# Row sums of attention weights: eight of sixteen key tiles summed on VectorE before TensorE

## The chip, the cores and the metric

One core of a Trainium2 chip runs the whole kernel. The metric is device time in microseconds (us), the median of three runs; lower is better. The engines named here are TensorE (PE; its weight loads are shown apart as PEld), VectorE (DVE), ScalarE (ACT), GpSimd (POOL), and SyncE (SP), whose queue issues all the kernel's DMAs.

## The reference

Eight entries (b), each of 2048 nodes with 256 features, go through two graph attention layers, each followed by a residual addition and a layer norm. In layer 0 there are 8 heads of 32 features:

```
e    = leaky_relu(e_src[i] + e_dst[j], 0.2) + softplus(beta) * log(adj + 1e-6)
attn = softmax over j of e, where adj[i, j] > 0
h    = attn @ x_proj                     (per head)
x    = layernorm(x + h @ W_out.T)
```

Layer 1 is dot-product attention on the result:

```
e = leaky_relu((x W1) (x W2).T, 0.2), masked by adj
x = layernorm(x + relu(softmax(e) @ (x W3)))
```

All data is float32. The softmax of layer 0 needs two things for each query i and head: the sum over all keys j of weight times value, and the sum over all keys of the weights alone, by which the first is divided.

## The kernel before

**Layer 0** (class `Gat`). Keys j are tiled by 128, so there are 16 key tiles (`jt`). Heads are taken in pairs (`hp`), so an entry has 4 passes of 16 key tiles, 64 units of work. In one unit (`step`) the mask-and-prior tile `mt` (128 keys by 2048 queries) is loaded; for each of the two heads VectorE makes a tile `s` = max(c, r) * mt, 128 x 2048, in one instruction (line 286); TensorE then multiplies `s` twice (line 294). With the values `v` as weights it adds to `val`, with the key's factor `e`, spread over 32 columns, it adds to `den`, the row sums. Each product is 128 x 32 by 128 x 512[...]; a unit has 8 for `val` and 8 for `den`. A float32 product appears as two instructions in the profile. `val` and `den` lie in PSUM over the whole pass. After the last key tile `finish` copies them out on ScalarE (lines 308 and 310), sends the row sums through DRAM to invert them (`rc`, `rec_d`) and to spread them (`rb`), and multiplies `ht` by them on VectorE (line 323), once for two passes.

**Buffers.** `s` has 4 tiles, that is two units; `mt` has 2, `c` has 3. The tag `d` has 2 tiles, which in the loop only `rb` uses (the adjacency tiles use it in entry 0).

**Layer 1** (class `Dot`). Queries are tiled by 128, so an entry has 16 dot steps. A step transposes the softmax tile `p` (line 404, copied by ScalarE to `pts`, line 406), makes the scores `e` of the next step (line 385), which ScalarE passes through Prelu into `p` (line 387), VectorE masks and reduces (line 390) and ScalarE exponentiates (line 391), and accumulates `acc` (line 420). Then `rec`, `z` and the layer norm follow. Every fourth step also makes the queries `h1` (`h1p`, line 374). The PSUM tiles of `e`, `pt` and the others are 3 in all; `acc` has one.

**The order.** The main loop runs layer 1 of one entry beside layer 0 of the next, and the order of TensorE is the order of the code. Units are put between the pieces of other work: 4 in `output` (layer 0's last product and its layer norm, by query tile), 8 in `turn` (transposes and `h3`), 4 in dot step 0 and then 4, 4, 3, 4, 4, 3, ... in dot steps 1 to 13:

```
dot.step(lambda k: layer_0((2, 1, 1)[k]))
for i in range(NT - 3):
    dot.step(lambda k: layer_0((0, 2 - (i % 3 == 2), 2)[k]))
```

Here k = 0 stands at the start of the step, 1 after the scores and 2 after `acc`. Dot steps 14 and 15 run at the start of the next round, with `project` of the following entry. So pass 0 of an entry lies in `output`, `turn` and dot step 0, and passes 1 to 3 in dot steps 1 to 13. Entry 0 has no layer 1 beside it; entry 7's layer 1 ends the program alone. The order on the other engines and on SP's queue is fixed when the program is built, by the tile framework's scheduler[...].

Of the kernel before, what the change touches and what calls it, by code (L numbers as in the profile page):

```python
# [9 lines left out]
F32 = mybir.dt.float32  # L10
BF16 = mybir.dt.bfloat16
I32 = mybir.dt.int32
AF = mybir.ActivationFunctionType
ALU = mybir.AluOpType
# [4 lines left out]
P = 128  # L19
# [8 lines left out]
def kernel(  # L28
# [26 lines left out]
    nc = tc.nc  # L55
    B, N, D = x.shape
    H, _, DH = w_proj.shape
    NT = N // P
    KC = D // P
    BK = 512  # L60
    NB = N // BK
    HALF = N // 2
    HP = 2
    NP = H // HP
    IG = BK // P

    const = ctx.enter_context(tc.tile_pool(name="const", bufs=1))
    dram = ctx.enter_context(tc.tile_pool(name="dram", bufs=1, space=DRAM))
# [7 lines left out]
    def mm_tile(name):  # L76
        return ps.tile([P, BK], F32, tag="mm", name=name)

    def wide_tile(name, tag, bufs, dtype=F32):
        return wide.tile([P, N], dtype, tag=tag, name=name, bufs=bufs)  # L80
# [7 lines left out]
    make_identity(nc, ident)  # L88
    eps_prior = const.tile([P, 1], F32)
    nc.vector.memset(eps_prior, PRIOR_EPS)  # L90
    eps_ln = const.tile([P, 1], F32)
    nc.vector.memset(eps_ln, LN_EPS)

# [61 lines left out]
    def make_mt(jt):  # L155

        a = wide.tile([P, NT, P], I32, tag="d", name="adj_t", bufs=2)
        nc.sync.dma_start(a, adj[:, ts(jt, P)].rearrange("(t p) j -> p t j", p=P))
        m = wide.tile([P, NT, P], F32, tag="p", name="m", bufs=2)
        nc.vector.tensor_scalar(m, a, 0.0, None, ALU.max)  # L160
        nc.scalar.activation(m, m, AF.Ln, bias=eps_prior)
        nc.scalar.activation(m, m, AF.Exp, scale=beta_c)
        nc.vector.scalar_tensor_tensor(m, a, 0.0, m, ALU.is_gt, ALU.mult)
        mt = wide_tile("mt", "mt", 2)
        for g in range(NB):
            t = mm_tile("mtp")
            for k in range(IG):
                nc.tensor.transpose(t[:, ts(k, P)], m[:, g * IG + k, :], ident)
            nc.scalar.copy(mt[:, ts(g, BK)], t)
        nc.sync.dma_start(mt_d[ts(jt, P), :], mt)  # L170
        return mt

    def load_mt(jt):
        mt = wide_tile("mt", "mt", 2)
        nc.sync.dma_start(mt, mt_d[ts(jt, P), :])
        return mt
# [25 lines left out]
    class Gat:  # L202
# [8 lines left out]
        def project(self):  # L211
# [8 lines left out]
            def turn(g):  # L220
                xr = chunk.tile([P, IG, D], F32, tag="xr", name="xr", bufs=1)
                nc.sync.dma_start(xr, xb[:, ts(g, IG), :])
                xt = chunk.tile([P, KC, BK], F32, tag="ht", name="xt", bufs=3)
                for kc in range(KC):
                    t = mm_tile("tr")
                    for k in range(IG):
                        nc.tensor.transpose(t[:, ts(k, P)], xr[:, k, ts(kc, P)], ident)  # L227
                    nc.scalar.copy(xt[:, kc, :], t)
                xts.append(xt)

            turn(0)
            for g in range(NB):
                if g + 1 < NB:
                    turn(g + 1)
                for k in range(IG):
                    it = g * IG + k
# [33 lines left out]
        def step(self, count=1):  # L270

            for _ in range(count):
                hp, jt = next(self.units)
                if jt == 0:
                    self.cs = [self.query_rows(hp * HP + a) for a in range(HP)]
                    self.val = pacc.tile([P, HALF], F32, tag="val", name="val")
                    self.den = pacc.tile([P, HALF], F32, tag="den", name="den")
                first = self.b == 0 and hp == 0
                while first and len(self.mts) < min(jt + 2, NT):
                    self.mts.append(make_mt(len(self.mts)))  # L280
                mt = self.mts[jt] if first else load_mt(jt)
                s = []
                for a in range(HP):
                    h = hp * HP + a
                    sa = wide_tile("s", "s", 4)
                    nc.vector.scalar_tensor_tensor(sa, self.cs[a], self.r[:, jt, h:h + 1], mt, ALU.max, ALU.mult)  # L286
                    s.append(sa)
                for dst in (self.val, self.den):
                    for c in range(HALF // BK):
                        for q in range(4):  # L290
                            h = hp * HP + q % 2
                            w = (self.v[:, jt, ts(h, DH)] if dst is self.val
                                 else self.e[:, jt, h:h + 1].to_broadcast([P, DH]))
                            nc.tensor.matmul(dst[ts(q, DH), ts(c, BK)], w,  # L294
                                             s[q % 2][:, ds(q // 2 * HALF + c * BK, BK)],
                                             start=(jt == 0), stop=(jt == NT - 1))
                if jt == NT - 1:
                    self.finish(hp)

        def finish(self, hp):  # L300


            b, lo = self.b, hp % 2 * HP * DH
            if lo == 0:
                self.hts.append(whole.tile([P, N], F32, name=f"ht{hp // 2}"))
            ht = self.hts[-1]
            for s in range(2):
                nc.scalar.copy(ht[lo:lo + HP * DH, ts(s, HALF)], self.val[ts(s, HP * DH), :])  # L308
            dn = chunk.tile([P, HALF], F32, tag="xr", name="dn", bufs=1)
            nc.scalar.copy(dn, self.den)  # L310
            rc = small.tile([P, HALF // DH], F32, name="rc", bufs=1)
            for q in range(4):
                nc.sync.dma_start(rc[ts(q, DH), :], dn[q * DH:q * DH + 1, :])
            nc.vector.reciprocal(rc, rc)
            nc.sync.dma_start(rec_d[b, hp].rearrange("q (p c) -> (q p) c", c=HALF // DH), rc)
            if lo == 0:
                return
            rb = wide_tile("rb", "d", 2)
            for a in range(2 * HP):
                src = rec_d[b, hp - 1 + a // HP, a % HP::HP, :]  # L320
                nc.sync.dma_start(rb[ts(a, DH), :].rearrange("p (s i) -> p s i", s=2),
                                  bass.AP(tensor=src.tensor, offset=src.offset, ap=[[0, DH]] + list(src.ap)))
            nc.vector.tensor_mul(ht, ht, rb)
# [176 lines left out]
```

## Time and profile before

| | |
|---|---|
| median of 3 runs | 4947.42 us (4947.27 to 4948.94) |
| profiled execution, its own time | 4950.43 us |
| its span, first to last instruction | 4948.7 us |
| mean granted TensorE clock | 0.965 |
| PE busy | 4550.1 us, 92% |
| DVE busy | 3042.8 us, 61% |
| ACT busy | 1671.8 us, 34% |
| DMA | 166 GB/s mean, 47.6% of 16 engines' span |

A line of the costliest groups gives source line, engine, operation, the tile written and those read, their shapes and the number of instructions; then busy time, the mean of one in ns, and the idle time of the engine just before them with what ended most of it. A line of a timeline gives the start, the length in us, then engine, line, operation and number of instructions merged, and in brackets the idle time before it and what ended it. Matmuls are pipelined, so that one's length overlaps the next's start; their pace is read from start to start.

### The profile page before, as it was taken

Reading aid. Unit: us, or ns where it says so; the run is one execution under the profiler, and the core shown is the slowest. Engines: PE = TensorE matmul, PEld = TensorE weight load, DVE = VectorE, ACT = ScalarE, POOL = GpSimd, SP = SyncE. Lnnn points to the kernel's source line nnn. Section 1 sums busy time; section 2 is a strip of 40 time slices with the busy share of each in tenths; the row PEclk is TensorE's granted clock in tenths of the full one; section 3 lists DMA queues with packets and bytes.
Section 4 is the critical chain, followed back from the end, with each engine's and each line's share of the span. In section 5 each row is a group of like instructions: output and inputs, shape, how many; then the busy total and the mean of one; then the engine's idle time right before and its main releaser. Section 6 shows DMA issues by size and latency. Waiting matters only on the chain. (4 is left out here: it accounts for less than half of the span.)

```text
span 4948.7 us, 64738 instructions
## 1 busy us (share of the span) xinstructions
PE 4550.1 (92%) x27164; PEld 2315.8 (47%) x27164; DVE 3042.8 (61%) x2316; ACT 1671.8 (34%) x3683; POOL 3.6 (0%) x14
## 2 busy tenths in 40 slices
PE   6777899988999799997999889998899979999899
PEld 3211444453544444544444444445444444444566
DVE  5888666647666376664676556664666637666222
ACT  5300333333333333334333333333333333333454
POOL 0000000000000000000000000000000000000000
PEclk8899899999999899998999999999999989999999
DMA  7787445435454455444554445443545435444111
GB/s 217 253 307 258 168 169 177 174 103 200 168 179 169 135 177 179 173 161 142 175 179 167 141 159 178 169 171 119 183 171 181 172 130 184 168 174 164 53 50 43
DMA packets 249013, 821.08 MB, mean 166 GB/s; under 512 B 33424, under 2 KB 150416, under 8 KB 172944
## 3 DMA queue, kind: packets, MB, share of 16 engines
q1 hardware_dynamic: 248720, 816.93, 47.6%
q8 instruction: 213, 3.49, 0.3%
q14 instruction: 80, 0.66, 0.0%
HBM read 756.55 MB, written 59.77 MB: 165 GB/s over the span
## 5 line engine op out<-in xcount | busy, mean ns | idle before, releaser
L286 DVE SCALAR_TENSOR_TENSOR s<-c,r,mt 128x2048 f32<-128x2048 f32 x1024 | 2349.5, 2345 | 447.7 <-PE den L294 348.4
L294 PE MATMUL val<-s,v 128*32 128x512 f32 x8192 | 1085.6, 614 | 163.3 <-DVE s L286 155.1
L294 PE MATMUL den<-s,e 128*32 128x512 f32 x8192 | 1047.2, 599 | 8.6 <-ACT dn L310 8.6
L420 PE MATMUL acc<-h,pts 128*128 128x256 f32 x4096 | 948.6, 380 | 2.3 <-ACT pts L406 2.3
L385 PE MATMUL e<-x1t,h 128*128 128x512 f32 x2048 | 904.3, 595 | 0.0
L420 PEld LDWEIGHTS acc<-h,pts 128*128 128x128 f32 x4096 | 749.2, 190 | 89.2 <-ACT pts L406 4.2
L294 PEld LDWEIGHTS val<-s,v 128*32 128x32 f32 x8192 | 245.4, 111 | 800.7 <-issue 525.2
L390 DVE CUSTOM_DVE_ANT_0 p<-p,pen 128x2048 f32<-128x2048 f32 x128 | 293.4, 2292 | 501.2 <-ACT p L387 501.2
L406 ACT COPY pts<-pt 128x512 f32<-128x512 f32 x512 | 298.2, 584 | 878.9 <-PE pt L404 878.2
L385 PEld LDWEIGHTS e<-x1t,h 128*128 128x128 f32 x2048 | 380.2, 191 | 449.6 <-issue 422.5
L294 PEld LDWEIGHTS den<-s,e 128*32 128x32 f32 x8192 | 286.7, 112 | 639.3 <-issue 621.2
L387 ACT ACTIVATE p<-e 128x512 f32<-128x512 f32 x512 | 305.4, 596 | 539.5 <-PE e L385 539.5
L428 DVE TENSOR_TENSOR z<-z,x1r 128x256 f32<-128x256 f32 x128 | 54.5, 426 | 482.3 <-ACT z L427 482.3
L404 PEld LDWEIGHTS pt<-ident,p 128*128 128x128 f32 x2048 | 239.6, 141 | 211.5 <-issue 176.7
L391 ACT ACTIVATE p<-p,neg 128x2048 f32<-128x2048 f32 x128 | 256.8, 2006 | 234.5 <-DVE neg L390 234.3
L404 PE MATMUL pt<-ident,p 128*128 128x128 f32 x2048 | 317.5, 278 | 5.2 <-ACT p L391 5.2
L355 PE MATMUL h3p<-w3s,x1t 128*128 128x256 f32 x512 | 147.1, 411 | 41.3 <-ACT x1t L351 41.3
L427 ACT ACTIVATE z<-acc,rec 128x256 f32<-128x256 f32 x128 | 60.6, 473 | 354.7 <-PE acc L420 354.7
L192 ACT ACTIVATE f<-mv,eps_ln 128x1 f32<-128x1 f32 x256 | 74.3, 290 | 309.8 <-DVE mv L190 309.2
L308 ACT COPY ht<-val 64x1024 f32<-64x1024 f32 x64 | 64.2, 1003 | 305.4 <-PE val L294 305.0
L357 ACT COPY h<-h3p 128x256 f32<-128x256 f32 x128 | 47.5, 371 | 318.4 <-PE h3p L355 287.4
L227 PE MATMUL tr<-ident,xr 128*128 128x128 f32 x256 | 47.6, 348 | 105.2 <-DMA xr<-in_x_dram 104.6
(76 smaller groups left out, 2027.0 us busy)
## 6 DMA issues: line engine op xcount, KB each, us to landing
mt<-mt_d SPq DMA_DIRECT2D x496, 1024.0 KB, 4.8
c<-c_d SPq DMA_DIRECT2D x64, 1024.0 KB, 6.2
pen<-pen_d SPq DMA_DIRECT2D x128, 512.0 KB, 3.4
xr<-in_x_dram SPq DMA_DIRECT2D x32, 512.0 KB, 3.9
adj_t<-in_adj_dram SPq DMA_DIRECT2D x16, 1024.0 KB, 7.1
h<-in_x_dram SPq DMA_DIRECT2D x32, 512.0 KB, 4.6
mt_d<-mt SPq DMA_DIRECT2D x16, 1024.0 KB, 5.4
adj_r<-in_adj_dram SPq DMA_DIRECT2D x16, 1024.0 KB, 8.3
```

The lines of the kernel that those rows point to most:

```text
L192: nc.scalar.activation(f[:, 0:1], mv[:, 1:2], AF.Ln, bias=eps_ln)
L286: nc.vector.scalar_tensor_tensor(sa, self.cs[a], self.r[:, jt, h:h + 1], mt, ALU.max, ALU.mult)
L294: nc.tensor.matmul(dst[ts(q, DH), ts(c, BK)], w, s[q % 2][:, ds(q // 2 * HALF + c * BK, BK)], start=(jt == 0), stop=(jt == NT - 1))
L308: nc.scalar.copy(ht[lo:lo + HP * DH, ts(s, HALF)], self.val[ts(s, HP * DH), :])
L355: nc.tensor.matmul(t[:, 0:D], x1t[:, kc, ts(it, P)], w3s[:, kc, :], start=(kc == 0), stop=(kc == KC - 1))
L385: nc.tensor.matmul(t, self.h1[:, kc, ts(it % IG, P)], self.x1t[:, kc, ts(c, BK)], start=(kc == 0), stop=(kc == KC - 1))
L387: nc.scalar.activation(p[:, ts(c, BK)], t, AF.Prelu, alpha=ALPHA)
L390: nc.vector.tensor_tensor_reduce(p, p, pen, -1.0, FMAX, ALU.add, ALU.min, neg)
L391: nc.scalar.activation(p, p, AF.Exp, bias=neg, scale=-1.0, accum_out=den)
L404: nc.tensor.transpose(t[:, ts(k, P)], p[:, ts(g * IG + k, P)], ident)
L406: nc.scalar.copy(pt, t)
L420: nc.tensor.matmul(acc, now[:, ts(k, P)], self.h3[:, j, :], start=(j == 0), stop=(j == NT - 1))
```

## The change

In entries 1 to 7 the row sums of key tiles 2 to 9 of every pass are no longer formed by TensorE tile by tile. For tile 2, ScalarE writes `s` times the key's factor `e` into a tile `d` for each head; for tiles 3 to 9, VectorE adds `s` times `e` to it, in place. At key tile 11, after that tile's own products, one row-sum product with a weight tile of ones takes the two sums into `den`. Tiles 0, 1 and 10 to 15 keep their row-sum product, and entry 0 keeps all. The two sum tiles come from the tag `d`, which `rb` uses too.

```diff
+    SUMMED = range(2, 10)
...
+    ones = const.tile([P, DH], F32)
+    nc.vector.memset(ones, 1.0)
...
-                for dst in (self.val, self.den):
-                    for c in range(HALF // BK):
-                        for q in range(4):
-                            h = hp * HP + q % 2
-                            w = (self.v[:, jt, ts(h, DH)] if dst is self.val
-                                 else self.e[:, jt, h:h + 1].to_broadcast([P, DH]))
-                            nc.tensor.matmul(dst[ts(q, DH), ts(c, BK)], w,
-                                             s[q % 2][:, ds(q // 2 * HALF + c * BK, BK)],
-                                             start=(jt == 0), stop=(jt == NT - 1))
+                v, e = self.v, self.e
+                heads = [hp * HP + a for a in range(HP)]
+                self.products(self.val, jt, [v[:, jt, ts(h, DH)] for h in heads], s)
+                if self.b > 0 and jt in SUMMED:
+                    if jt == SUMMED[0]:
+                        self.sums = [wide_tile("d", "d", 2) for _ in heads]
+                        for d, sa, h in zip(self.sums, s, heads):
+                            nc.scalar.activation(d, sa, AF.Copy, scale=e[:, jt, h:h + 1])
+                    else:
+                        for d, sa, h in zip(self.sums, s, heads):
+                            nc.vector.scalar_tensor_tensor(d, sa, e[:, jt, h:h + 1], d, ALU.mult, ALU.add)
+                else:
+                    self.products(self.den, jt, [e[:, jt, h:h + 1].to_broadcast([P, DH]) for h in heads], s)
+                if self.b > 0 and jt == SUMMED[-1] + 2:
+                    self.products(self.den, jt, [ones] * HP, self.sums)
                 if jt == NT - 1:
                     self.finish(hp)
+
+        def products(self, dst, jt, weights, s):
+            for c in range(HALF // BK):
+                for q in range(4):
+                    nc.tensor.matmul(dst[ts(q, DH), ts(c, BK)], weights[q % 2],
+                                     s[q % 2][:, ds(q // 2 * HALF + c * BK, BK)],
+                                     start=(jt == 0), stop=(jt == NT - 1))
```

## The prediction

> **What bounds the kernel now.** I read the page's busy shares first, then the costliest groups, the chain, and last the timelines of one stage.
>
> ```profile
> PE 4550.1 (92%) x27164; PEld 2315.8 (47%) x27164; DVE 3042.8 (61%) x2316; ACT 1671.8 (34%) x3683; POOL 3.6 (0%) x14
> ...
> PE 5%; ACT 0%; DVE 0%; issue 0%
> ...
> L286 DVE SCALAR_TENSOR_TENSOR s<-c,r,mt 128x2048 f32<-128x2048 f32 x1024 | 2349.5, 2345 | 447.7 <-PE den L294 348.4
> L294 PE MATMUL val<-s,v 128*32 128x512 f32 x8192 | 1085.6, 614 | 163.3 <-DVE s L286 155.1
> L294 PE MATMUL den<-s,e 128*32 128x512 f32 x8192 | 1047.2, 599 | 8.6 <-ACT dn L310 8.6
> ```
>
> TensorE (PE) is busy 92%, VectorE (DVE) 61%, and DVE's largest wait is for PE to give back an s buffer. The chain is followed only through the last 5%, so it says nothing of the loop. These are averages; the timeline of one dot step with four units (entry 1), on PE and then on DVE, shows the beat:
>
> ```profile
> 1463.73 0.66 PE L404 MATMUL pt<-ident,p 128*128 128x128 f32 x4
> 1464.23 7.03 PE L385 MATMUL e<-x1t,h 128*128 128x512 f32 x16
> 1471.19 1.92 PE L294 MATMUL val<-s,v 128*32 128x512 f32 x16
> 1472.93 1.90 PE L294 MATMUL den<-s,e 128*32 128x512 f32 x16
> 1474.65 1.90 PE L294 MATMUL val<-s,v 128*32 128x512 f32 x16
> 1476.36 1.90 PE L294 MATMUL den<-s,e 128*32 128x512 f32 x16
> ...
> 1493.57 0.66 PE L404 MATMUL pt<-ident,p 128*128 128x128 f32 x4
> ```
>
> ```profile
> 1471.92 2.29 DVE L390 CUSTOM_DVE_ANT_0 p<-p,pen 128x2048 f32<-128x2048 f32 x1 [2.36 <-ACT p L387]
> 1474.14 0.08 DVE L390 DVE_READ_ACCUMULATOR2_ANT neg<- 128x1 f32 x1
> 1474.88 9.14 DVE L286 SCALAR_TENSOR_TENSOR s<-c,r,mt 128x2048 f32<-128x2048 f32 x4 [0.66 <-PE den L294]
> ```
>
> PE starts pieces without a gap; the step lasts 1493.57 - 1463.73 = 29.84 us. A unit is val 1.72 + den 1.72 = 3.44 us by start times. Without its four units a step is 29.84 - 13.76 = 16.1: pt 0.44 + e 7.0 ahead, the pt/acc block (7.9) between units, the rest rounding. A three-unit step is 29.84 - 3.44 = 26.4. Every fourth step has h1p, 3.44 more. DVE makes the s pair of one unit in 9.14 / 2 = 4.57 us. In such a step it is busy 21.7 us: 18.3 for s, 2.37 for p with its read-out, 1.2 for z, st, mv, rec.
>
> [...] the timelines above follow program order. [...] at two starts of the same eleven matmuls:
>
> ```profile
> 302.58 1.49 PE L294 MATMUL val<-s,v 128*32 128x512 f32 x11 [1.22 <-DVE s L286]
> ...
> 310.55 2.78 PE L294 MATMUL val<-s,v 128*32 128x512 f32 x11 [2.87 <-DVE s L286]
> ```
>
> After the longer gap they take 2.78 instead of 1.49, and normal pace is back about 5 us later: roughly 2 us lost per gap.
>
> **The change, part by part.** It touches 7 entries x 4 passes = 28 passes. PE loses 8 den sets of 16 per pass and gains one ones set, net 7 x 1.72 = 12.0 us per pass, 337 us in all. DVE gains 7 tiles x 2 heads per pass, 392 instructions of 2.285, 896 us; nearest row is L286 itself, also f32 from two f32 tensors with a per-partition scalar. ACT gains two scaled copies per pass of 2.0 us (as L391's exp), 112 us on an engine 34% busy; they fit between its waits for PE except as noted. The ones memset is once, nothing. No DMA is added, but the sums take both d buffers until the ones product, so the rb load waits for that; built order puts rb's loads four units after it, and their last two wait for rec_d anyway. I take 0 here, up to 2 us per two passes. New waits: PE's ones product waits for tile 9's sums, but DVE has those behind it before it makes the s of tile 11, so PE waits for that s anyway. ACT's copy waits for its s tile and a free d buffer; in pass 2 the second copy waits for the rb multiply, and two Prelu stand behind it, and behind them p and PE's e: I count 2 us, which the DVE queue covers. If ACT is later than that, p and then pt are late next.
>
> PE's relief is real only where PE sets the pace. A summed unit now costs PE 1.72 and DVE 9.14. The built order on DVE is s pair, sum pair, s pair, sum pair, with p and z between, so PE cannot get the next s before the sum ahead of it. The s ring has 4 tiles, two units: DVE's lead is at most two pairs. So each summed run is a DVE-bound stretch, and the DVE time saved in the unsummed tiles cannot be banked. I follow DVE through each run in the built order, starting where the ring first lets it start, until PE leads again (units numbered through an entry; pass = 16 units).
>
> *Pass 0*, output and turn. In entry 1, DVE has its output-stage work behind it at 1155.9. Then 7 sum pairs (tiles 3 to 9) and 8 s pairs (4 to 11) = 15 x 4.57 = 68.6: s of unit 11 at 1224.7, of unit 10 at 1220.1. PE: unit 10 to 1223.5, two turn rounds 3.1, unit 11 + ones + last h3p 3.44 + 1.72 + 0.97, end 1232.8. Before, this was 1212.2. **+20.6**.
>
> *Pass 1*, dot steps 1 to 4. From the step's start s of unit 18 can begin at 10.9 (pt, e, unit 16). To the s of unit 26: 9 s pairs, 7 sum pairs = 73.1, two p 4.7, two z groups 2.4: 91.1; about 0.5 is lost at z and p, 91.7. Then PE alone: unit 26 3.44, pt + e 7.4, units 27 and 28 with ones 8.6, acc 7.9, two units 6.9 = 34.3: 126.0. Before: 4 x 29.84 (or 26.4 + 3.44) = 119.4. **+6.6**.
>
> *Pass 2*, steps 5 to 8. s of unit 35 begins at 25.7. To s of unit 43: 9 + 7 pairs 73.1, three p 7.1, rb multiply 2.3, two z 2.4 = 84.9: 110.6. PE: unit 43 + ones 5.2, acc 7.9, two units 6.9: 130.6. Before 29.84 + 26.4 + 33.3 + 29.84 + 1 at the pass change = 120.4. **+10.2**.
>
> *Pass 3*, steps 9 to 13. DVE is free for p of step 11 at 35.8 (step 10's e, with Prelu delayed some 1 us by a scaled copy queued between). To s of unit 58: 8 + 7 pairs 68.6, three p 7.1, two z 2.4: 113.9; unit 59's s at 118.6, then unit + ones 5.2 and step 13 at 29.1: 152.9. Before 146.5. **+6.4**.
>
> Sum 43.8 per entry, 306.6 for seven. In each stretch PE now idles about 7 us at a time (a summed unit needs 9.14, or 11.5 with p). Cold restarts inside the stretch are hidden by DVE; those at its end, three per entry, are not: 3 x 2 = 6 per entry, 42 in all; bounds are 0 and 10 per entry. Total +348: span 4948.7 + 348 = 5297. The profiled execution (4950.4) was 3 us above the median, so 5294.
>
> **Rivals.** *Pooled*: if lead could be carried from unsummed to summed tiles, the dot steps 1 to 13 would cost only DVE's sum: 48 units x 4.57 = 219.4, 21 sum pairs 96.0, 13 x 3.6 = 46.8, together 362 against 119.4 + 120.4 + 146.5 = 386 before, -24; with turn's +20.6, -3.5 per entry, -25 in all: about 4920. For it: the DVE total still fits. Against: it needs a lead of some 17 us, the deficit of step 2 (DVE 40.1, PE 23.0), and the ring holds 9.1; it decides only from four units of lead. *Cheap sums*: break-even needs the sum pair to fall from 4.57 to about 3, as +43.8 spreads over 28 pairs; L163, an in-place f32 form, takes 2286 each, so about 4947 is unlikely. *Half absorbed*: shorter stalls and no cold clock, +70 to +290: 5020 to 5240. *Order trouble*: reciprocals and layer norms sit behind sums on DVE, ACT waits in order for them, and e fills its three PSUM tiles behind late Prelu. I found only about 1 us of this per stretch; at 4 us for each of four stretches it gives +112 more: 5370 to 5480.
>
> **How the numbers follow.** A change under 0.2% cannot be told from none. My case (5240 to 5370) 0.62; half absorbed 0.18; order trouble 0.14; pooled 0.05; cheap sums 0.01. Range 5160 to 5410: it leaves out pooled and the lower part of half absorbed, and the far end of order trouble. Faster 0.05, same 0.01, slower 0.94.
>
> **What would show it.** Right: den matmuls 8192 down to 5056 in all with the ones product; DVE near 3940 us, 75% of the span; PE's wait for s, 155 before, grown to several hundred, in gaps of 5 to 8 us inside tiles 3 to 9; DVE without gaps there; dot steps of 36 to 40 us (2, 7 and 11) among others of 26 to 36; granted clock below 0.965; turn stage about 75 us instead of 54. Wrong: PE without gaps in summed tiles, sums well under 2.28 us, or long waits of ACT for rec or mv.

## The result

The change is slower. The kernel takes 5311.43 us (median of 4 runs, 5297.74 to 5321.97) against 4948.18 us before (4 runs, 4947.27 to 4950.48): a ratio of 1.073, with a 95% interval of 1.0707 to 1.0757, or 363 us. The forecast was 5294, with 5160 to 5410 as its range. The profiled execution took 5310.25 us with a span of 5308.5 us; the mean granted TensorE clock fell from 0.965 to 0.93.

The lines of the page after the change that answer to those of before: busy shares, then the groups (line, engine, operation, tiles, count, then busy time, mean of one in ns, and the idle time ahead with what ended most of it).

```profile
PE 4529.1 (85%) x24028; PEld 2253.2 (42%) x24028; DVE 3902.4 (74%) x2709; ACT 1756.1 (33%) x3739; POOL 3.6 (0%) x14
...
L289 DVE SCALAR_TENSOR_TENSOR s<-c,r,mt 128x2048 f32<-128x2048 f32 x1024 | 2360.2, 2343 | 234.7 <-PE den L312 129.2
L312 PE MATMUL val<-s,v 128*32 128x512 f32 x8192 | 1360.9, 670 | 543.8 <-DVE s L289 535.0
...
L301 DVE SCALAR_TENSOR_TENSOR d<-s,e,d 128x2048 f32<-128x2048 f32 x392 | 902.1, 2342 | 0.0
...
L312 PE MATMUL den<-s,e 128*32 128x512 f32 x4608 | 656.4, 605 | 8.6 <-ACT dn L326 8.6
```

The row-sum products fell from 8192 to 4608 plus 448 with ones. TensorE (PE) got idle time for them: it is idle 380.8 us longer than before and busy only 21.0 us less (its `val` products got longer, from 614 to 670 ns in the mean), and the difference is the 359.8 us by which the span grew. PE's wait for an `s` tile, from 155.1 to 535.0 us, is nearly all of that idle time. VectorE (DVE) waits less for PE than before (129.2 us, from 348.4) and never waits ahead of a sum: its share went from 61% to 74%, and the time it used to wait in is not enough, because of where it lies. The same step type as before, four units with pass 1's sums in them, first PE and then DVE (start, length, engine, line, operation, and in brackets the wait before it):

```profile
1344.14 0.66 PE L420 MATMUL pt<-ident,p 128*128 128x128 f32 x4
1344.63 7.03 PE L401 MATMUL e<-x1t,h 128*128 128x512 f32 x16
1351.59 1.92 PE L312 MATMUL val<-s,v 128*32 128x512 f32 x16
1354.76 1.04 PE L312 MATMUL val<-s,v 128*32 128x512 f32 x2 [1.25 <-DVE s L289]
1359.23 3.25 PE L312 MATMUL val<-s,v 128*32 128x512 f32 x14 [3.43 <-DVE s L289]
1362.42 0.66 PE L420 MATMUL pt<-ident,p 128*128 128x128 f32 x4
```

```profile
1347.84 4.61 DVE L301 SCALAR_TENSOR_TENSOR d<-s,e,d 128x2048 f32<-128x2048 f32 x2
1352.36 2.34 DVE L289 SCALAR_TENSOR_TENSOR s<-c,r,mt 128x2048 f32<-128x2048 f32 x1
1354.63 2.28 DVE L406 CUSTOM_DVE_ANT_0 p<-p,pen 128x2048 f32<-128x2048 f32 x1
1356.84 0.08 DVE L406 DVE_READ_ACCUMULATOR2_ANT neg<- 128x1 f32 x1
1356.84 2.34 DVE L289 SCALAR_TENSOR_TENSOR s<-c,r,mt 128x2048 f32<-128x2048 f32 x1
1359.10 4.61 DVE L301 SCALAR_TENSOR_TENSOR d<-s,e,d 128x2048 f32<-128x2048 f32 x2
```

Before, it was DVE that carried a wait here and PE that ran without a gap; now it is the reverse. PE has finished a unit's `val` at 1353.5 and needs the next `s` pair. DVE starts that pair at 1352.36, since the sums of an earlier tile stand ahead of it; the first head's tile lets two matmuls start at 1354.76, then the reduction of `p` stands between the two heads, and the second head's tile comes at 1359.2. Two sums take 4.52 us from start to start (1347.84 to 1352.36), so 2.26 each. At the head of this run, for the `s` pairs of units 18 and 19, DVE had to wait for PE to give back a tile:

```profile
1328.88 9.14 DVE L289 SCALAR_TENSOR_TENSOR s<-c,r,mt 128x2048 f32<-128x2048 f32 x4 [0.66 <-PE den L312]
```

This start lies 11.15 us after the start of its step in each of the seven rounds. From there to the `s` of unit 26 DVE waits for no tile from PE any more: it enters the run held back by the ring of `s` tiles, and then falls behind PE.

To see which stage pays, the main loop's rounds are cut at its landmarks. Means over the rounds, in us (the first stage without the first round, in which it is shorter); the first column runs from the start of `project` to the first `h1p` and holds `project`, steps 14 and 15, the output and the turn; pass 1 is dot steps 1 to 4, pass 2 is 5 to 8, and pass 3 is 9 to 13 with the wait up to the start of the next `project`. (The stretch left out, from the first `h1p` to step 1, holds step 0 and the last four tiles of pass 0. It takes 40.5 us before and after.)

| | with pass 0 | pass 1 | pass 2 | pass 3 | sum of differences |
|---|---|---|---|---|---|
| before | 153.1 | 119.4 | 121.5 | 156.0 | |
| after | 173.8 | 127.4 | 136.8 | 163.4 | |
| difference | +20.8 | +7.9 | +15.3 | +7.5 | +51.4 |
| forecast, without cold clock | +20.6 | +6.6 | +10.2 | +6.4 | +43.8 |

Seven entries times 51.4 is 360, which is the whole difference of the two spans. One round as windows of the trace, before and then after: the stretch, its length, the busy time (and instructions) of PE, PEld, DVE, ACT and POOL, the granted clock, the DMA share and GB/s. The rows are the four stages of the table.

```profile
2239.83:2392.78 152.95, 130.14 (x754) 76.34 (x754) 84.57 (x89) 55.01 (x196) 0.36 (x1) 0.91 0.45 156
2433.23:2552.67 119.44, 119.44 (x749) 58.36 (x745) 81.37 (x55) 38.07 (x70) 0.00 (x0) 1.00 0.46 156
2552.67:2674.18 121.51, 119.85 (x749) 58.15 (x745) 84.78 (x57) 38.98 (x69) 0.00 (x0) 1.00 0.50 178
2674.18:2830.00 155.82, 146.12 (x909) 71.75 (x905) 96.59 (x67) 50.31 (x88) 0.00 (x0) 0.98 0.47 161
```

```profile
2385.34:2558.72 173.38, 131.19 (x642) 73.31 (x643) 117.71 (x104) 58.09 (x198) 0.37 (x1) 0.88 0.41 138
2599.17:2726.63 127.46, 116.66 (x637) 55.97 (x633) 111.82 (x69) 41.16 (x72) 0.00 (x0) 0.95 0.43 146
2726.63:2865.93 139.30, 122.77 (x637) 56.72 (x633) 115.38 (x71) 42.13 (x71) 0.00 (x0) 0.91 0.44 155
2865.93:3030.08 164.15, 144.09 (x797) 69.35 (x793) 127.07 (x81) 52.98 (x90) 0.00 (x0) 0.94 0.44 153
```

In passes 1 and 2 of before PE is busy but for 1.7 us, and its clock is 1.00. After, DVE is busy 111.82 of 127.46 us in pass 1, and 30 us more than before. Pass 2 is odd in one thing: with 112 matmuls fewer PE is busy longer (122.77, from 119.85), at a clock of 0.91.

### The profile page after: what moved, and what is told of

The parts are those of the page before. It is cut to its first block, busy times and chain, and to the rows that moved or that the text cites. A ratio compares the mean times of both kernels' runs of the same rounds, so it can differ in the third digit from the quotient of the medians.

```text
span 5308.5 us, 58877 instructions
## 1 busy us (share of the span) xinstructions
PE 4529.1 (85%) x24028; PEld 2253.2 (42%) x24028; DVE 3902.4 (74%) x2709; ACT 1756.1 (33%) x3739; POOL 3.6 (0%) x14
## 5 line engine op out<-in xcount | busy, mean ns | idle before, releaser
L289 DVE SCALAR_TENSOR_TENSOR s<-c,r,mt 128x2048 f32<-128x2048 f32 x1024 | 2360.2, 2343 | 234.7 <-PE den L312 129.2
L312 PE MATMUL val<-s,v 128*32 128x512 f32 x8192 | 1360.9, 670 | 543.8 <-DVE s L289 535.0
L301 DVE SCALAR_TENSOR_TENSOR d<-s,e,d 128x2048 f32<-128x2048 f32 x392 | 902.1, 2342 | 0.0
L312 PEld LDWEIGHTS val<-s,v 128*32 128x32 f32 x8192 | 268.6, 116 | 1395.7 <-DVE s L289 830.8
L436 PEld LDWEIGHTS acc<-h,pts 128*128 128x128 f32 x4096 | 751.7, 191 | 96.9 <-ACT pts L422 10.1
L312 PE MATMUL den<-s,e 128*32 128x512 f32 x4608 | 656.4, 605 | 8.6 <-ACT dn L326 8.6
L312 PEld LDWEIGHTS den<-s,e 128*32 128x32 f32 x4608 | 178.0, 114 | 376.9 <-issue 359.5
L420 PE MATMUL pt<-ident,p 128*128 128x128 f32 x2048 | 329.0, 285 | 5.2 <-ACT p L407 5.2
L371 PEld LDWEIGHTS h3p<-w3s,x1t 128*128 128x128 f32 x512 | 91.6, 199 | 126.7 <-ACT x1t L367 59.5
```

Source lines behind the costliest of these rows:

```text
L301: nc.vector.scalar_tensor_tensor(d, sa, e[:, jt, h:h + 1], d, ALU.mult, ALU.add)
L312: nc.tensor.matmul(dst[ts(q, DH), ts(c, BK)], weights[q % 2], s[q % 2][:, ds(q // 2 * HALF + c * BK, BK)], start=(jt == 0), stop=(jt == NT ...
L371: nc.tensor.matmul(t[:, 0:D], x1t[:, kc, ts(it, P)], w3s[:, kc, :], start=(kc == 0), stop=(kc == KC - 1))
L420: nc.tensor.transpose(t[:, ts(k, P)], p[:, ts(g * IG + k, P)], ident)
L436: nc.tensor.matmul(acc, now[:, ts(k, P)], self.h3[:, j, :], start=(j == 0), stop=(j == NT - 1))
```

## The experiments

My theory was that of the forecast: a run of summed tiles is bound by DVE, because the ring of four `s` tiles lets DVE be two units ahead at most; what PE is spared in those tiles is worth nothing, and a cold TensorE clock adds a little. The rivals were that the sums' total load costs the time, wherever they stand; that leaving the row-sum products out doesn't help at all, or the ones product or the copies cost it; and that the clock is the main cost. The first four kernels were timed beside the kernel before at 4943.63 us, the next four at 4944.26, the last at 4946.75. (In the expectations e2 is the kernel with unused sums, e4 the one with seven spread tiles, e7 the one with five.) Where no interval is given, a kernel was run once; the four runs of the change lie between 5297.74 and 5321.97, so differences of some ten us against it are not to be read closely. All diffs are against the changed kernel.

**One part alone: the relief.** Row-sum products left out, no sums in their place.

```diff
-                    if jt == SUMMED[0]:
-                        self.sums = [wide_tile("d", "d", 2) for _ in heads]
...
-                            nc.vector.scalar_tensor_tensor(d, sa, e[:, jt, h:h + 1], d, ALU.mult, ALU.add)
+                    pass
...
-                if self.b > 0 and jt == SUMMED[-1] + 2:
-                    self.products(self.den, jt, [ones] * HP, self.sums)
```

> Leaves out the row-sum products of key tiles 2 to 9 in entries 1 to 7 and makes no sums in their place, so the row sums lack half of the keys: PE's relief alone. My theory (PE sets the pace of the kernel before, and the loss comes from VectorE's sums alone): 28 passes x 8 x 1.72 = 385 us less than before, some of it lost where two units of val follow each other in 3.4 us and the ring of s must be refilled in 9.1: 4565 to 4620 us. Rival (the relief is worth little since something else than PE, such as the s pairs or the p chain, already sets the pace): above 4750.

4598.4 us, 345 below before and inside its range. Passes 1 to 3 fall by 13.7, 13.2 and 13.7 us; eight products of 1.72 are 13.8, so PE's relief shows nearly in full in the dot steps where nothing else is added. In the first stage 10.1 of it shows. So PE is the bound of the kernel before in the dot steps, and for the most part in the first stage, and the relief is real.

**The other part alone: the sums.** All row-sum products are kept; the sums are made and not used.

```diff
-                else:
-                    self.products(self.den, jt, [e[:, jt, h:h + 1].to_broadcast([P, DH]) for h in heads], s)
-                if self.b > 0 and jt == SUMMED[-1] + 2:
-                    self.products(self.den, jt, [ones] * HP, self.sums)
+                self.products(self.den, jt, [e[:, jt, h:h + 1].to_broadcast([P, DH]) for h in heads], s)
```

> Keeps all row-sum products of the kernel before and makes the sums on ScalarE and VectorE beside them, unused (no ones product): VectorE's load alone. My theory (in the summed run VectorE alone sets the pace, so PE's relief is worth nothing there): the four stretches are as long as with the change, less 1.72 for each ones product, and PE idles in shorter gaps: 5220 to 5290 us, slightly below the 5311 of the change. Rival (the change's PE relief of 337 us counts, and the sums cost some 700 us): about 5650.

5209.6 us, some 10 under the range, and 102 *below* the change, although PE does 3136 matmuls more. Its page:

```profile
PE 4674.9 (90%) x27164; PEld 2321.5 (45%) x27164; DVE 3899.9 (75%) x2709; ACT 1761.3 (34%) x3739; POOL 3.6 (0%) x14
...
L309 PE MATMUL val<-s,v 128*32 128x512 f32 x8192 | 1203.1, 624 | 289.9 <-DVE s L289 281.4
```

DVE's work is that of the change to 3 us (3899.9 and 3902.4), PE fills with products what it waited away before (281.4 us of waits for `s`, from 535.0), and the time does not rise with them. So in these stretches PE's work is free, and removing it gains nothing. The 102 us that are left can be the ones product, which the change has and this kernel has not, and the clock; the kernel with a busy PE, below, parts them.

**The sums' length halved.** Each sum runs over half of the columns.

```diff
-                            nc.vector.scalar_tensor_tensor(d, sa, e[:, jt, h:h + 1], d, ALU.mult, ALU.add)
+                            nc.vector.scalar_tensor_tensor(d[:, 0:HALF], sa[:, 0:HALF], e[:, jt, h:h + 1], d[:, 0:HALF], ALU.mult, ALU.add)
```

> The change with each VectorE sum over half the queries only (1024 elements, about 1.22 us instead of 2.29), the other half of the sums left out. My theory (chain of s and sum pairs in each stretch): 7 pairs x 2.1 us = 15 us off each of the four stretches of an entry, -15 per entry against the kernel before, with some cold clock left: 4840 to 4890 us. Rival (the loss comes from waits, buffers, ScalarE's copies or the order of the queues and not from the sums' length): above 5150.

4886.1 us, inside the range: 425 below the change.

```profile
L301 DVE SCALAR_TENSOR_TENSOR d<-s,e,d 128x1024 f32<-128x1024 f32 x392 | 484.7, 1274 | 0.0
```

Half a sum takes 1.274 us in the mean. (The 1.22 expected is an estimate: it lies on the straight line between two rows of before, 426 ns for 256 columns at L428 and 2289 for 2048 at L323.) The sums' busy time fell by 902.1 - 484.7 = 417 us and the kernel by 425. The likeness of the two numbers is in part chance, since the granted clock rose as well, from 0.93 to 0.959. Against the kernel with a busy PE, below, whose clock is 0.96, the stages are 45.0 + 8.8 = 53.8 us per entry shorter, for 417 / 7 = 59.6 us less of sums: most of a sum is on the path. ScalarE's copies and the ones product are all in this kernel, which is faster than before, so these alone don't make the loss. It also gives an estimate of the price at which the change as written would break even, by a straight line between two points. The pair costs 4.68 by its mean (2 x 2342) at +51.4 us per entry, and 2.55 at -8.8: 28 us per entry for each us of a pair, so break-even is near 2.9; the forecast had about 3.

**The same sums, spread.** Seven tiles are summed, every other one from 1 to 13, instead of eight in a run; the first is ScalarE's copy, so DVE makes six pairs of sums per pass, not seven.

```diff
-    SUMMED = range(2, 10)
+    SUMMED = range(1, 14, 2)
...
-                if self.b > 0 and jt == SUMMED[-1] + 2:
+                if self.b > 0 and jt == SUMMED[-1] + 1:
```

> Seven tiles summed, but every other one (1, 3, ..., 13) instead of a run, ones product at tile 14. My theory (the loss is from the run of summed tiles, which a ring of two units cannot bridge; alternating tiles need a lead of one unit only): VectorE 351 us and PE about 357 us in dot steps 1 to 13 of an entry against 386 before, turn +1 to +5: -15 to -28 per entry, 4750 to 4845 us. Rival (VectorE's total load and its fixed order cost the time wherever the sums stand): about 5170, the price of seven tiles in a run.

4835.33 us (4831.83 to 4839.23), 0.9782 of before with an interval of 0.9766 to 0.9799: *faster* than before by 108 us, near the upper end of its range. The page, and PE's timeline at two summed tiles of pass 1:

```profile
PE 4343.4 (90%) x24476; PEld 2236.6 (46%) x24476; DVE 3763.3 (78%) x2653; ACT 1764.9 (37%) x3739; POOL 3.6 (0%) x14
...
L312 PE MATMUL val<-s,v 128*32 128x512 f32 x8192 | 1160.4, 619 | 262.1 <-DVE s L289 254.0
```

```profile
1318.03 3.64 PE L312 MATMUL val<-s,v 128*32 128x512 f32 x32
1321.49 1.90 PE L312 MATMUL den<-s,e 128*32 128x512 f32 x16
1323.32 0.66 PE L420 MATMUL pt<-ident,p 128*128 128x128 f32 x4
1323.82 7.03 PE L401 MATMUL e<-x1t,h 128*128 128x512 f32 x16
1330.78 2.76 PE L312 MATMUL val<-s,v 128*32 128x512 f32 x18
1333.73 1.49 PE L312 MATMUL val<-s,v 128*32 128x512 f32 x11 [0.19 <-DVE s L289]
```

Two units' `val` stand next to each other with one row-sum product behind them. At the first of the two places (`val` x32) PE doesn't wait; at the second it waits 0.19 us, after two matmuls that the first head's tile allowed. But the kernel differs from the change in two things, the place of the sums and their number, so the next one was needed.

**The same seven in a run.**

```diff
-    SUMMED = range(2, 10)
+    SUMMED = range(2, 9)
```

> Seven tiles in a run (2 to 8) instead of eight, ones product at tile 10: the control for e4, which sums seven tiles too. My theory (a run pays for its chain): about 5 us less per pass than the change, 28 passes: 5150 to 5190 us, some 330 above the same seven tiles spread (4835). Rival (the number of tiles, not their place, decides): near 4835.

5210.6 us, 20 above its range. Against the spread kernel it has the same 336 sums, the same 5056 row-sum products of tiles and 448 of ones (the ones product at tile 10, and at 14 in the spread kernel), and each was timed beside before at 4944. They are 375 us apart. PE's waits for `s` (total, times, longest) in the run, then in the spread kernel:

```profile
PE val L312 <- DVE s L289: 478.1, 265, 13.7
```

```profile
PE val L312 <- DVE s L289: 254.0, 146, 13.8
```

So it is the place of the sums and not their load. The miss has a location: shortening the run by one tile took 5.4, 5.0 and 2.4 us off passes 1 to 3, but only 1.0 off the first stage. Why pass 0 and pass 3 give back so little was not tried.

**A busy PE beside the same sums.** All row-sum products kept, and the ones product too, so that tiles 2 to 9 count twice in the row sums. DVE's work is that of the change, and PE has more to do.

```diff
-                else:
-                    self.products(self.den, jt, [e[:, jt, h:h + 1].to_broadcast([P, DH]) for h in heads], s)
+                self.products(self.den, jt, [e[:, jt, h:h + 1].to_broadcast([P, DH]) for h in heads], s)
```

> The change with the removed row-sum products of tiles 2 to 9 put back beside the sums, so that tiles 2 to 9 count twice in the row sums: more work for PE, the same chain on VectorE. My theory (of the 102 us by which e2 was faster than the change, 28 x 1.72 = 48 are the ones product and some 54 the cold clock that longer gaps bring): 5250 to 5270 us, below the 5311 of the change although PE does 385 us more. Rival (the ones product was hidden and the whole 102 us is clock): 5205 to 5220. Rival (no clock effect, e2 gained otherwise): 5300 or more.

5267.0 us, as expected: 44 us *faster* than the change, with 3584 matmuls (28 passes x 8 x 16, some 385 us of PE at 1.72 a product) more. Its windows, the same four stages of the same round:

```profile
2370.51:2543.33 172.82, 140.59 (x769) 77.49 (x770) 117.52 (x104) 58.12 (x198) 0.37 (x1) 0.90 0.40 139
2583.79:2710.90 127.11, 123.91 (x764) 59.05 (x760) 112.04 (x69) 41.24 (x72) 0.00 (x0) 0.99 0.42 147
2710.90:2843.38 132.48, 126.19 (x764) 58.97 (x761) 115.19 (x71) 42.36 (x71) 0.00 (x0) 1.00 0.46 163
2843.38:3005.43 162.05, 149.27 (x925) 72.21 (x921) 126.89 (x81) 53.42 (x90) 0.00 (x0) 0.98 0.44 155
```

DVE's busy time is that of the change within 0.3 us in every row; the clock is 0.99, 1.00 and 0.98 in passes 1 to 3, where the change has 0.95, 0.91 and 0.94; and pass 2 is 6.8 us shorter. Over all rounds the stages differ from before by +19.7, +7.9, +11.0 and +6.4, together 45.0. So the cold clock (stretches in which the granted clock is low) costs the change about 44 us, an eighth of the loss, if the added products cost nothing. They aren't free everywhere: in pass 1 of this round the `s` of unit 26 was ready at 2674.75, and PE took it up at 2675.80, since it still had unit 25's row-sum product to do, which the change leaves out. So 44 is rather too low than too high, give or take the spread of the change's runs. 57 us is what lies between this kernel and the one with unused sums, that is, the ones product and what hangs on it (28 x 1.72 = 48 for the product alone): the four stages differ by 1.6, 2.4, 1.7 and 1.9 us, each near one product. The clock as the main cost is out.

**Fewer, wider spread.** Five tiles, every third, and six tiles.

```diff
-    SUMMED = range(2, 10)
+    SUMMED = range(1, 14, 3)
```

> Five tiles, every third (1, 4, 7, 10, 13), ones product at tile 14. My theory: PE is relieved of 4 x 1.72 = 6.9 us per pass and VectorE follows with a lead of one or two units, so nearly all of 28 x 6.9 = 193 us is kept: 4750 to 4785 us, faster than e4 although less is taken from PE. Rival (more relief is better as long as the tiles are spread): above 4835.

```diff
-    SUMMED = range(2, 10)
+    SUMMED = (1, 3, 6, 8, 11, 13)
```

> Six tiles, spread (1, 3, 6, 8, 11, 13), ones product at tile 14. My theory: 5 x 1.72 = 8.6 us per pass of relief, some of it lost in the turn stage, where VectorE is already near PE's pace: 4765 to 4810 us, between e7 and e4. Rival (more relief is better): above 4835 is excluded by it, and it would lie above e7 only if e7 lies above e4.

Both also have the ones product one tile after the last sum. Both miss: 4844.15 us, 0.9794 of before (0.9779 to 0.9808), and 4844.06, 0.9793 (0.9776 to 0.9809), no better than seven, from which the intervals don't part them. I had reckoned that with fewer sums DVE would fit everywhere, and PE's net relief (four products of 1.72 per pass with five tiles, 6.9 us) would show in all four passes. It shows for the most part in the dot steps: -5.3, -7.2 and -4.5 us with five tiles. There the rival was right, and more relief is better: in the profiled executions passes 1 to 3 together change by -17.1 us with five tiles, -19.3 with six and -21.2 with seven, though a smaller share of the relief is kept each time (of 20.6, 25.8 and 31.0 us by products of 1.72). The first stage, though, got *longer*, by 3.3 and 4.0 us, and by 5.1 with seven, which eats the difference. With five tiles the output part of it takes 34 us instead of 31 in most rounds, and the turn is not shorter; with six and seven it is the turn that grows, from 54.0 to 57.0 to 58.4 and to 58.8. So spread sums help in the dot steps and hurt in pass 0, in all three spreads. Where it is lost is shown; which wait it is was not settled.

**Spread, in the dot steps only.** From this follows a last version: seven tiles spread in passes 1 to 3, pass 0 as before.

```diff
-    SUMMED = range(2, 10)
+    SUMMED = range(1, 14, 2)
...
-                if self.b > 0 and jt in SUMMED:
+                if self.b > 0 and hp > 0 and jt in SUMMED:
...
-                if self.b > 0 and jt == SUMMED[-1] + 2:
+                if self.b > 0 and hp > 0 and jt == SUMMED[-1] + 1:
```

> As e4 (every other tile, 1 to 13), but only in passes 1 to 3 of an entry, which run beside the dot steps; pass 0, in the output and turn stages, is as before the change. My theory (in output and turn the sums gain nothing, +5 us per entry in e4, while steps 1 to 13 keep their gain): e4's dot steps 375 us with turn and output as before 153, against 158: some 5 us per entry or 35 us less than e4: 4785 to 4815 us. Rival (pass 0 gained in e4 too, by what follows it): 4835 or more.

4811.69 us (4808.37 to 4815.24), 0.9724 of before (0.9708 to 0.974), inside its range: the fastest of the kernels that form the whole row sums, 2.8% below before and 9.4% below the change. Two windows of it, the stage with pass 0 and pass 1:

```profile
2181.52:2334.27 152.75, 129.51 (x754) 76.01 (x755) 84.58 (x89) 55.02 (x196) 0.36 (x1) 0.91 0.46 156
...
2374.72:2487.35 112.63, 111.36 (x653) 55.41 (x649) 108.14 (x67) 39.78 (x68) 0.00 (x0) 1.00 0.47 164
```

The first stage is back at its time of before (152.95 there). In pass 1 PE is busy 111.36 and DVE 108.14 of 112.63 us: both are nearly full, and this is what the change wanted. A relief of six products is 10.3 us, and 6.8 come out of it. Nearly all of the rest lies at two places in the pass where the second unit of two comes late: PE does two matmuls with the first head's tile alone and then waits 0.19 and 1.09 us for the second one, so that the three and four products up to the next `pt` take 6.5 and 9.1 us instead of 5.3 and 7.0. DVE, with 4.5 us left in the pass, has become nearly as much of a bound as PE.

A deeper ring (six or eight `s` tiles) would test the depth of the ring directly, and `d` tiles of their own for the sums would show what sharing them with `rb` costs; neither was tried. That the ring's depth sets how long a run may be is argued from the built order, from DVE's wait for a tile at the head of the run and from the spread's success, not shown by a change of the depth.

## Why the prediction was right, and where its steps were off

**The bound and the mechanism: right.** PE paced the kernel before (relief alone: -345 us), and in a run of summed tiles DVE does (half sums: -425 us; the same seven tiles spread instead of in a run: -375 us). The timeline after the change shows what the sums do to the work behind them: the `s` pair that PE waited for started at 1352.36, the moment the sums ahead of it (4.52 us for the two) ended.

**The DVE chain: right within 3%, in part by luck.** The forecast's +20.6, +6.6, +10.2 and +6.4 per entry, 43.8, are to be held against the kernel with a busy PE: +19.7, +7.9, +11.0 and +6.4, 45.0. In pass 1 the walk said that the `s` of unit 26 would be ready 91.7 us after the start of step 1; it was ready after 89.6 to 91.5 in the seven rounds of the change. The tail after it was too short: an `acc` block was priced at 7.9, but in the kernel before it takes 8.4 with the `pt` that opens it (1478.19 to 1486.57), and the forecast had put such remainders down to rounding. The kernel with a busy PE adds a wait of about 1 us of its own in this pass. Errors from -0.9 to +1.3 us in four stages make a sum that fits better than its parts. The sum was priced at 2.285 and takes 2.26 from start to start.

**Pass 2: mis-sized, 10.2 against 15.3.** Of this 0.8 shows in the busy-PE kernel too. There were two errors: the stretch on DVE began 28.9 us after step 5's start and not 25.7, so that the `s` of unit 43 came at 111.8 there and not at 110.6 (at 113.1 in the first two rounds of the change); and the waits at the pass change are 2.07 (step 5 of before is 31.91 long, not 29.84), where I counted 1, so that the pass of before takes 121.5 and not 120.4. The first adds to the loss, the second takes from it, and little is left. The other 4.3 is the clock, as far as the two kernels differ in nothing else.

**The cold clock: the sum right, its place wrong.** I took 6 us per entry, at the ends of the stretches, and held that cold restarts inside a stretch are hidden by DVE. Measured are 51.4 - 45.0 = 6.4, but 4.3 of it is in pass 2 alone, and it is inside the stretch. That the total fits is luck: the term was right in size for another reason than the one given. Two rounds that follow each other show how it gets in: the same `pt` and `h1p` in pass 2, warm in the first and cold in the second, and then DVE's reduction of `p` in the two steps that follow.

```profile
1505.58 0.66 PE L420 MATMUL pt<-ident,p 128*128 128x128 f32 x4
1506.08 3.60 PE L390 MATMUL h1p<-x1t,w 128*128 128x512 f32 x8
...
2141.38 1.12 PE L420 MATMUL pt<-ident,p 128*128 128x128 f32 x4
2142.29 4.27 PE L390 MATMUL h1p<-x1t,w 128*128 128x512 f32 x8
```

```profile
1517.29 2.29 DVE L406 CUSTOM_DVE_ANT_0 p<-p,pen 128x2048 f32<-128x2048 f32 x1 [0.85 <-ACT p L403]
...
1552.32 2.29 DVE L406 CUSTOM_DVE_ANT_0 p<-p,pen 128x2048 f32<-128x2048 f32 x1 [0.31 <-ACT p L403]
...
2154.18 2.29 DVE L406 CUSTOM_DVE_ANT_0 p<-p,pen 128x2048 f32<-128x2048 f32 x1 [2.11 <-ACT p L403]
...
2191.81 2.29 DVE L406 CUSTOM_DVE_ANT_0 p<-p,pen 128x2048 f32<-128x2048 f32 x1 [1.76 <-ACT p L403]
```

Cold, `h1p` ends later, so do the scores and ScalarE's `p`, and DVE, the bound of the stretch, waits 2.11 instead of 0.85 us with its whole queue behind it, and in the next step 1.76 instead of 0.31. With a wait of 1.08 for ScalarE's `z` between the two, which the warm round doesn't have, that is 3.8 of some 5 us; the rest comes at the end of the stretch. So DVE hides a slow `val`, but not a slow product whose result DVE itself waits for. Pass 2 takes 133.8 to 134.1 us in the three rounds where `h1p` takes its 3.60 us, and 138.4 to 139.3 in the four where it takes 3.86 to 4.37; in the kernel with a busy PE it is 132.5 in all seven. Why the same instructions are warm in one round and cold in another can be read from the clock of the two rounds just before `h1p` (windows of the trace, as above):

```profile
1501.93:1505.34 3.41, 3.14 (x14) 0.58 (x14) 3.41 (x3) 0.00 (x0) 0.00 (x0) 0.50 0.55 202
1505.34:1508.76 3.42, 3.42 (x14) 1.75 (x12) 3.42 (x3) 1.17 (x2) 0.00 (x0) 1.00 0.26 108
...
2133.40:2136.80 3.40, 1.04 (x2) 0.14 (x2) 3.40 (x2) 0.00 (x0) 0.00 (x0) 1.00 0.00 1
2136.80:2140.22 3.42, 2.40 (x11) 0.58 (x14) 3.42 (x3) 0.00 (x0) 0.00 (x0) 0.50 0.42 110
2140.22:2143.63 3.41, 3.41 (x12) 1.59 (x7) 3.41 (x3) 0.59 (x1) 0.00 (x0) 0.50 0.50 202
```

In this trace the granted clock is either 1.00 or 0.50, and every change lies on one grid with a step of 3.413 us (of 108 slow stretches 39 last one step and 50 two). PE's waits ahead of `h1p` are the same in both rounds (3.14 and 1.22 us), but they lie otherwise on that grid: in the first the slow stretch is 3.41 us long and ends before `h1p` starts at 1506.08, in the second it is 6.83 us long and reaches 1.3 us into it. All seven rounds go by this: `h1p` is slow in the four in which the slow stretch reaches it. In the trace of before, the eleven matmuls that the forecast compared have a granted clock of 1.00 where they take 1.49 us (from 302.58, after a wait of 1.22) and of 0.50 where they take 2.78 (from 310.55, after a wait of 2.87). Over the series the clock goes with PE's gaps too: it is 0.93 with them and 0.96 with PE kept busy beside the same DVE work. In both rounds shown the slow stretch begins during the wait of 1.22 us, after a step of the grid in which PE is busy 1.04 of 3.4 us (in the second, the row that starts at 2133.40). How long a gap has to be for it was not tested.

**The gaps: wrong in form.** I said gaps of 5 to 8 us. The 316 waits for `s` last 1.7 us in the mean (535.0 / 316): two matmuls start with the first head's tile, so a gap falls in two, 1.25 and 3.43 in the step shown. Only 7 of them are over 5 us, and none of these lies in a run of summed tiles.

**What else was said would show:** DVE near 3940 us and 75% (3902.4, 74%), PE's wait for `s` at several hundred (535.0), the turn near 75 us (73.1 to 76.2, from 54.0), clock below 0.965 (0.93): all so. DVE runs nearly without gaps there (in the run that starts at 1328.88 it waits once, 1.77 us for `p`). Steps of 36 to 40 us at 2, 7 and 11 hold for the first two rounds (36.8, 38.5, 39.1); over all rounds they go from 35.1 to 36.8, 38.5 to 41.5 and 39.1 to 40.9.

**The rivals.** *Pooled* fell: its gain needs the sums' load to be what counts, and the same load costs 375 us more in a run than spread. Its premise that the DVE total fits was sound: with the sums spread, the dot steps gain. *Cheap sums* fell on the sum's measured length, 2.26 us. (L163, taken as its likeness, reads an int32 tile beside its f32 one; the price held all the same.) *Half absorbed* had no cold clock and shorter stalls; the first would have been worth about 44 us, and the stalls are not shorter. *Order trouble* at 4 us a stretch fell: with the clock kept up, no stage is more than 1.3 us above the walk.

## What to carry to other kernels

Work moved from a full engine to a half-idle one can cost time though the totals fit: here the buffers between the two hold two units, one summed tile between two others gained, and eight in a row cost 7%. That the depth of the buffers sets the limit is argued, not tested. Before moving work, walk through one stretch with the queue in order and not through the totals, and then spread the moved work so that each stretch as long as the ring is balanced for itself. Leave out the stage in which it doesn't pay even so (here pass 0).

## What was not expected of the hardware

More work made the kernel faster: with 3584 matmuls added that change nothing of DVE's work, it took 5267.0 us instead of 5311.4, because PE's gaps were filled and its granted clock stayed at 0.96 instead of 0.93. Most of the price of the cold clock (4.3 of 6.4 us per entry) was paid in pass 2, where a chain leads from the cold engine back to the one that was the bound. Most of that was paid in four rounds of seven, with the same instructions in each: what differs is where PE's waits fall on the 3.413 us grid on which this trace's clock changes.
